# First cross attention: the mask product in 32-column tiles, and in two of eight rounds a multiplication on VectorE

## The chip, the cores and the metric

The kernel runs on one core of a Trainium2 chip. The metric is the device time of one execution in microseconds, as the median of several runs. The engines of the core are called PE (TensorE; PEld is its weight load), DVE (VectorE), ACT (ScalarE), POOL (GpSimd) and SP (the queue that issues the DMAs).

## The reference, cut to what matters

The model has two layers (cross attention, a mixing block, a feed-forward block, each twice in different forms) on 2 x 256 tokens of width 256. The change touches only the first cross attention: 256 queries of each batch attend to 4096 context rows, with 16 heads of width 16, under a mask of the form 256 x 4096 that all heads share.

```python
q = proj(q_vec, Wq, bq); k = proj(k_vec, Wk, bk); v = proj(v_vec, Wv, bv)   # 16 heads of 16
energy = einsum('bhqd,bhkd->bhqk', q, k) / sqrt(16)
energy = where(mask_input == 0, -1e9, energy)
attn = softmax(energy, axis=-1)
context = einsum('bhqk,bhkd->bhqd', attn, v)
```

A masked weight can be made in two ways: a very large negative number is added to the score ahead of the exponential, or the weight is multiplied by 0 after it. The mask of this case has only ones, so nothing is masked, but the kernel does the work for any mask.

## The kernel before, in words

`l0_xattn` (from line 153) holds the first cross attention. Its work is a software pipeline over units: one unit `u` is one batch and one pair of heads (16 units). Per unit the kernel makes two passes over the context. The first pass finds each query's largest masked score, the second makes the weights and weighs the values with them.

The main loop (from line 616) counts rounds `g`, eight per unit, and each round has two half-steps (`for a in range(2)`), one for each head of the pair. A half-step does the following, in this order on PE:

- what the generators in the list `slow` have to give: projections of keys (`project_k`, bank `psK`) and values (`project_v`, `psV`), the maxima turned into a row (`take_max`, `psM`), the division by the sum (`collect`, `psC`) and others. These are matmuls on the full 128 x 128 array. Many half-steps have none of them;
- `weights_part`, first piece (line 423): the mask product. The identity matrix `identb` (bf16) is loaded, and `addT[:, j]` (0 or -3e38 for each key and query, bf16) streams through it, so that the mask lands in PSUM bank `sts[0]`;
- `max_part` (line 408) for unit `u` and the rest of `weights_part` for the unit that is ten rounds behind, interleaved. All of these use the array in row tiles of 32 rows: the scores of the first pass into the double bank `st`, the subtraction of the maximum (line 430, a product of ones `oneb` with the three-part row `msh`) and the scores of the second pass (line 440) into two banks `sT`, one for each value of `h`, on top of the mask;
- `weigh` (line 459) for the round before: four products, one for each 32-column tile of the array, of the values with the weights `p`, into `av`.

`h` here is no head: it parts the 512 keys of a round `j` into two halves of 256. The half `h = 0` has its mask added by the mask product. The half `h = 1` has it multiplied in after the exponential: POOL multiplies `p[:, 1]` by `keep[:, j]` (line 451), and in the last ten rounds, where there is no first pass any more, DVE does it (line 449, `on_vector`).

The other engines in a half-step: ACT takes the exponential of both banks (line 446, `h = 0` first). DVE runs `max_out` (line 417), a fused add of the mask and maximum over the 128 x 1024 scores in `st`, and with it frees `st`.

What sets the order: the tile framework is told to keep each engine's instructions in the order in which the program issues them (a manual schedule), so each engine is one queue in order of the code. The buffers that couple the engines are `st` (two double banks), the pool of three single banks from which `sT` (two per half-step), `psK`, `psV`, `psM`, `psC` are taken in rotation, and `p` (five buffers).

`addT` and `keep` are made once, in the first rounds, by DVE in `make_masks` (lines 342 and 344), from mask pieces that SP loads two ahead.

Of the kernel before, what the change touches and what calls it, by code (L numbers as in the profile page):

```python
# [15 lines left out]
ALU = mybir.AluOpType  # L16
AX = mybir.AxisListType

P = 128
# [7 lines left out]
BIG = 3.0e38  # L27
# [18 lines left out]
class Kernel:  # L46
# [106 lines left out]
    def l0_xattn(self):  # L153
        nc, T, tc = self.nc, self.T, self.tc
# [95 lines left out]
        addT = a1.tile([P, NJ, 2, S], BF16, name="addT")  # L250
# [16 lines left out]
        for j in range(NJ):  # L267
# [3 lines left out]
            if j == 2:  # L271
                for f in range(2):
                    ps = self.bank("psQ")
                    for k in range(2):
                        nc.tensor.matmul(
                            ps, lhsT=wq[:, k, f * P : (f + 1) * P], rhs=self.xnT[:, k, :], start=k == 0, stop=k == 1
# [34 lines left out]
        def load_rest():  # L311
            nc.sync.dma_start(sel, T["x0_sel"])
            nc.sync.dma_start(wo, T["x0_wo"])
            self.bcast_load(bv, T["x0_bv"])
            self.bcast_load(bo, T["x0_bo"])
            nc.sync.dma_start(cw, T["a0_small"])
# [5 lines left out]
            nc.vector.memset(t, 0.0)  # L322


        NADD = 1
        none = a1.tile([P, 2], F32, name="none")

        def make_masks():
            def piece(n):
                j, h = divmod(n, 2)  # L330
                mi = a2.tile([P, 2, S], I32, name="mi", tag="mi", bufs=3)
                nc.sync.dma_start(mi, T["x0_maskT"][:, j, 2 * h : 2 * h + 2])
                return mi

            ahead = [piece(0), piece(1)]
            for n in range(2 * NJ):
                j, h = divmod(n, 2)
                if n + 2 < 2 * NJ:
                    ahead.append(piece(n + 2))
                yield  # L340
                if h == 0:
                    nc.vector.tensor_scalar(addT[:, j], ahead[n], 0, -BIG, ALU.is_equal, ALU.mult)
                else:
                    nc.vector.tensor_scalar(keep[:, j], ahead[n], 0, None, ALU.not_equal)

            for qc in range(2):
                nc.vector.tensor_reduce(
                    none[:, qc : qc + 1], madd[:, qc].rearrange("p c h a k -> p (c h a k)"), AX.X, ALU.max
                )
                yield  # L350
            nc.vector.tensor_scalar(none, none, -1.0, None, ALU.is_lt)
# [63 lines left out]
        def max_out(st, mx, par, qc, c):  # L415
            junk = a2.tile([P, 2, 512], BF16, name="junk", tag="junk", bufs=1)
            nc.vector.tensor_tensor_reduce(  # L417
                out=junk, in0=st, in1=madd[:, qc, c].rearrange("p h a k -> p h (a k)"), scale=1.0, scalar=-1e38,
                op0=ALU.add, op1=ALU.max, accum_out=mx[:, 2 * qc + par, c : c + 1],
            )  # L420

        def weights_part(qz, kst, msh, par, j, p, sts, on_vector):
            nc.tensor.matmul(  # L423
                sts[0], lhsT=self.identb, rhs=addT[:, j].rearrange("p a q -> p (a q)"), start=True, stop=False,
                skip_group_check=True,
            )
            yield
            for h in range(2):
                r = 64 * h + 32 * par
                nc.tensor.matmul(  # L430
                    sts[h], lhsT=oneb[r : r + 3, :], rhs=msh[r : r + 3, :].unsqueeze(1).to_broadcast([3, 2, S]),
                    start=h >= NADD, stop=False, tile_position=(r, 0), skip_group_check=True,
                )
            yield
            for a in range(2):
                for i in range(2):
                    for h in range(2):
                        r = 64 * h + 32 * par
                        n0 = j * S + a * P
                        nc.tensor.matmul(  # L440
                            sts[h][:, a * S : (a + 1) * S], lhsT=kst[r : r + 32, n0 : n0 + P], rhs=qz[r : r + 32, i, :],
                            start=False, stop=i == 1, tile_position=(r, 0), skip_group_check=True,
                        )
                yield
            for h in range(2):
                nc.scalar.activation(p[:, h].rearrange("p a q -> p (a q)"), sts[h], AF.Exp)  # L446

            if on_vector:
                nc.vector.scalar_tensor_tensor(p[:, 1], p[:, 1], BIG, keep[:, j], ALU.min, ALU.mult)
            else:  # L450
                nc.gpsimd.tensor_tensor(p[:, 1].bitcast(I32), p[:, 1].bitcast(I32), keep[:, j], ALU.mult)  # L451

        def weigh(av, vf, p, hp, par, j):

            for h in range(2):
                for a in range(2):
                    c = 32 * (2 * h + a)
                    o = ((2 * h + a) * H + 2 * hp + par) * VD
                    nc.tensor.matmul(  # L459
                        av[c : c + 32, :], lhsT=vf[:, o : o + 32], rhs=p[:, h, a, :],  # L460
                        start=j == 0 and par == 0, stop=j == NJ - 1, tile_position=(0, c), skip_group_check=True,
                    )
# [91 lines left out]
        NU = B * NP  # L554
        mx, msh, avs, vf, cxo, pt = {}, {}, {}, {}, {}, {}
        av = self.ps3.tile([P, 2, S], F32, name="av", tag="av")

        def chain(gens):
            for g in gens:
                yield from g  # L560
# [36 lines left out]
        def masks():  # L597
            yield from rest_of_mask()
            yield from make_masks()
# [17 lines left out]
        for g in range(8 * NU + 12):  # L617
            u, i = divmod(g, 8)
            if i == 0 and u + 1 < NU:
                load_q(u + 1)  # L620
                load_k(u + 1, 0, NJ)
            if g == 12:
                load_rest()
            if g == 14:
                slow.append(second_batch())
            if g == 8 * NU - 28:
                self.begin_rest(slow, load_weight, load_row)
            if g == 8 * NU - 6:
                self.begin_first(slow)
            if g == 8 * NP + 4:  # L630
                slow.append(second_values())
            if g in (7 * NP, 13 * NP):
                slow.append(find_base(g // (8 * NP)))
            if u >= 1 and u <= NU and i == 0:
                msh[u - 1] = a2.tile([P, S], BF16, name="msh", tag="msh")
                slow.append(take_max(u - 1, mx[u - 1], msh[u - 1]))
            if u < NU and i == 0:
                mx[u] = self.sm.tile([P, 4, 4], F32, name="mx0", tag="mx0")
            u2, j = divmod(g - 10, 8)
            u3, j3 = divmod(g - 11, 8)  # L640

            for a in range(2):
                for s in list(slow):
                    if next(s, slow) is slow:
                        slow.remove(s)
                gens = []
                for n in ([a] if u < NU else [0, 1] if a == 0 else []) if 0 <= u2 < NU else []:
                    p = pt[u2, j, n] = a2.tile([P, 2, 2, S], F32, name="p", tag="p", bufs=5)
                    if u < NU or n == 0:
                        sts = [self.bank("sT") for _ in range(2)]  # L650
                    else:
                        pair = self.bank2("st")
                        sts = [pair[:, h, :] for h in range(2)]
                    part = weights_part(qz[u2], kst[u2], msh[u2], n, j, p, sts, u >= NU)
                    next(part)
                    gens.append(part)
                if u < NU:
                    st = self.bank2("st")
                    gens = [max_part(st, qz[u], kst[u], 1 - a, *divmod(i, 4)), *gens]
                interleave(*gens)  # L660
                if u < NU:
                    max_out(st, mx[u], 1 - a, *divmod(i, 4))
                if 0 <= u3 < NU:
                    b3, hp3 = divmod(u3, NP)
                    if j3 == 0 and a == 0:
                        avs[u3] = lk.tile([P, 2, S], F32, name="avs", tag="avs")
                    weigh(av[:, a, :], vf[b3, j3], pt.pop((u3, j3, a)), hp3, a, j3)
                    if j3 == NJ - 1:
                        (nc.vector.tensor_copy if u3 == NU - 1 and a else nc.scalar.copy)(avs[u3][:, a, :], av[:, a, :])  # L669
                        if a == 1:  # L670
                            todo = [collect(avs[u3], b3, hp3)]
                            if hp3 >= NP - 2:
                                todo.append((most_heads if hp3 == NP - 2 else last_heads)(b3))
                            slow.append(chain(todo))
# [1278 lines left out]
```

## Time and profile before

| | |
|---|---|
| median of 3 runs | 1053.68 us (1049.66 to 1055.73) |
| the profiled execution | 1050.14 us, its span 1048.4 us |
| mean granted PE clock in it | 0.965 |
| DVE `max_out`, L417 | 256 of 1223 ns, 313.0 us busy |
| POOL `keep` multiplication, L451 | 236 of 1285 ns, 302.7 us busy |
| ACT exponential, L446 | 492 of 595 ns, 267.2 us busy |
| PE mask product, L423 | 246 of 394 ns, 96.8 us busy |
| DVE `keep` multiplication, L449 | 20 of 687 ns, 13.4 us busy |

The first half-step's `st` begins at 47 us, the first mask product is seen at 91.5 us, the last half-step with a `max_out` begins at 590 us, and the weighing ends at 627 us. What follows is the rest of the first layer and the second layer, which the change does not touch.

How to read the rows: a row of the timeline gives the start in us from the start of the span, the time in us, the engine, the line of the kernel, the operation, the tiles written and read, the shapes, and how many instructions of one kind were put together. In brackets stands how long the engine was idle before it, and what ended that. "issue" is time in which the engine waited for nothing that the profile shows. A matmul's time holds its passage through the array, so that the times of matmuls which follow each other overlap. A few matmul records can be missing.

### The profile page before, as it was taken

How to read it: one execution, taken by the hardware profiler on the slowest of the kernel's cores; microseconds unless marked ns; L12 is line 12 of the kernel's file. 1: busy time of each engine (PE TensorE's matmuls, PEld its weight loads, DVE VectorE, ACT ScalarE, POOL GpSimd, SP SyncE). 2: the span in 40 equal slices, each digit the busy share in tenths (PEclk: the TensorE clock that was granted, in tenths of full speed). 3: DMA queues.
4: the chain of work that ended last, by engine and by line, in shares of the span. 5: the costliest groups of instructions: out<-in, count | busy, mean ns of one | idle time of the engine just before them, and what ended most of it. 6: DMA issues, size and time to landing. Idle time of an engine off the chain costs nothing.

```text
span 1048.4 us, 21101 instructions
## 1 busy us (share of the span) xinstructions
PE 966.5 (92%) x8384; PEld 581.7 (55%) x8390; DVE 672.3 (64%) x1315; ACT 480.1 (46%) x1009; POOL 386.8 (37%) x418
## 2 busy tenths in 40 slices
PE   6998899999999999999999989764999999997978
PEld 2654355555555665555555547543575676455745
DVE  3268956666677447777887797668565432877651
ACT  1533456666666344666566672223141121455511
POOL 3323477777777435777777400111000000000000
PEclk9998799999999999999999999986899999999999
DMA  8888344334432240222221009432253796000000
GB/s 290 265 246 269 100 113 122 109 95 131 112 92 49 65 126 27 51 53 52 52 62 42 2 3 366 160 102 83 79 178 94 249 410 211 1 1 1 1 1 21
DMA packets 57523, 117.57 MB, mean 112 GB/s; under 512 B 6224, under 2 KB 28880, under 8 KB 55376
## 3 DMA queue, kind: packets, MB, share of 16 engines
q1 hardware_dynamic: 57424, 116.22, 35.8%
q8 instruction: 66, 1.08, 0.4%
q14 instruction: 33, 0.27, 0.1%
HBM read 97.85 MB, written 18.35 MB: 111 GB/s over the span
## 4 chain that ended last, share of the span: by engine, by line
PE 81%; DVE 12%; ACT 2%; issue 2%; DMA 2%; POOL 1%; SPq 0%; POOLq 0%; DVEq 0%; ACTq 0%
PE av L459 12%; PE st L408 10%; PE sT L440 8%; PE sT L423 6%; PE psV L365 6%; PE psS L1339 5%; PE psK L201 5%; PE av L1371 5%; PE psP L1456 3%; DVE junk L417 2%; PE psC L472 1%; PE psO L1581 1%; PE psP L807 1%; PE psS L1504 1%; PE psT L1379 1%
## 5 line engine op out<-in xcount | busy, mean ns | idle before, releaser
L417 DVE CUSTOM_DVE_ANT_0 junk<-st,madd 128x1024 bf16<-128x1024 f32 x256 | 313.0, 1223 | 97.1 <-PE st L408 94.5
L451 POOL TENSOR_TENSOR p<-p,keep 128x512 int32<-128x512 int32 x236 | 302.7, 1285 | 135.5 <-ACT p L446 130.0
L446 ACT ACTIVATE p<-sT 128x512 f32<-128x512 f32 x492 | 267.2, 595 | 180.0 <-PE sT L440 169.0
L440 PE MATMUL sT<-qz,kst 32*128 32x256 f32 x1968 | 207.1, 328 | 0.0
L408 PE MATMUL st<-kst,qz 32*128 32x512 f32 x1024 | 190.6, 450 | 7.5 <-DVE mx L417 7.5
L459 PE MATMUL av<-p,v 128*32 128x256 f32 x2048 | 168.0, 395 | 3.3 <-ACT avs L669 2.4
L440 PEld LDWEIGHTS sT<-qz,kst 32*128 32x128 f32 x1968 | 155.7, 189 | 0.2
L408 PEld LDWEIGHTS st<-kst,qz 32*128 32x128 f32 x1024 | 78.0, 186 | 83.8 <-issue 64.2
L104 POOL TENSOR_TENSOR rsx<-ve,nhalf 128x1 f32<-128x1 f32 (+1 forms) x10 | 5.7, 574 | 276.8 <-DVE ve L103 276.8
L430 PE MATMUL sT<-msh,oneb 3*128 3x512 bf16 x492 | 100.4, 390 | 0.5 <-ACT msh L402 0.2
L423 PE MATMUL sT<-addT,identb 128*128 128x512 bf16 x246 | 96.8, 394 | 0.2 <-ACT p L446 0.2
L201 PE MATMUL psK<-ctx,wkv 128*128 128x512 f32 x128 | 66.4, 650 | 6.6 <-DMA ctx<-in_ctxT 6.6
L423 PEld LDWEIGHTS <-identb 128*128 128x128 bf16 x256 | 25.4, 101 | 80.2 <-issue 79.1
L188 POOL TENSOR_TENSOR part<-kf,part 128x512 f32<-128x512 f32 x32 | 41.9, 1309 | 70.2 <-DVE part L187 67.7
L459 PEld LDWEIGHTS av<-p,v 128*32 128x32 f32 x2048 | 42.9, 108 | 41.6 <-ACT avs L669 3.3
L365 PE MATMUL psV<-wkv,ctx 128*128 128x256 f32 x256 | 61.8, 389 | 0.0
L1371 PE MATMUL av<-w,pT 128*128 128x256 f32 x256 | 60.3, 381 | 1.1 <-ACT pT L1383 1.1
L1339 PE MATMUL psS<-w,qk 128*128 128x512 f32 x128 | 57.8, 603 | 0.0
L365 PEld LDWEIGHTS psV<-wkv,ctx 128*128 128x128 f32 x256 | 46.7, 190 | 15.0 <-issue 9.2
L187 DVE TENSOR_SCALAR part<-kf 128x512 int32<-128x512 int32 x32 | 13.6, 426 | 61.4 <-ACT kf L205 27.9
L1371 PEld LDWEIGHTS av<-w,pT 128*128 128x128 f32 x256 | 46.4, 190 | 7.3 <-ACT pT L1383 2.1
L205 ACT ACTIVATE kf<-psK,bqk 128x512 f32<-128x512 f32 x32 | 22.0, 688 | 51.7 <-PE psK L201 51.7
(308 smaller groups left out, 1265.8 us busy)
## 6 DMA issues: line engine op xcount, KB each, us to landing
ks<-part SPq DMA_DIRECT2D x64, 256.0 KB, 2.9
w<-in_m_w SPq DMA_DIRECT2D x32, 512.0 KB, 7.7
kst<-ks SPq DMA_DIRECT2D x30, 512.0 KB, 6.6
ctx<-in_ctxT SPq DMA_DIRECT2D x24, 512.0 KB, 4.6
w<-in_ctxT SPq DMA_DIRECT2D x16, 512.0 KB, 5.7
w<-in_ctx SPq DMA_DIRECT2D x16, 512.0 KB, 4.0
qz<-qs SPq DMA_DIRECT2D x64, 64.0 KB, 6.2
mi<-in_x_maskT SPq DMA_DIRECT2D x16, 256.0 KB, 4.2
```

The lines of the kernel that those rows point to most:

```text
L201: nc.tensor.matmul(ps, lhsT=w[:, 0, k, f * P : (f + 1) * P], rhs=ct[:, k, :], start=k == 0, stop=k == 1)
L365: nc.tensor.matmul(ps[:, i, :], lhsT=ct[:, k, n0 : n0 + P], rhs=w[:, 1, k, :], start=k == 0, stop=k == 1)
L408: nc.tensor.matmul(st[:, h, :], lhsT=qz[r : r + 32, i, qc * P : (qc + 1) * P], rhs=kst[r : r + 32, c * 512 : (c + 1) * 512], start=i == 0, ...
L417: nc.vector.tensor_tensor_reduce(out=junk, in0=st, in1=madd[:, qc, c].rearrange("p h a k -> p h (a k)"), scale=1.0, scalar=-1e38, op0=ALU. ...
L423: nc.tensor.matmul(sts[0], lhsT=self.identb, rhs=addT[:, j].rearrange("p a q -> p (a q)"), start=True, stop=False, skip_group_check=True,)
L430: nc.tensor.matmul(sts[h], lhsT=oneb[r : r + 3, :], rhs=msh[r : r + 3, :].unsqueeze(1).to_broadcast([3, 2, S]), start=h >= NADD, stop=Fals ...
L440: nc.tensor.matmul(sts[h][:, a * S : (a + 1) * S], lhsT=kst[r : r + 32, n0 : n0 + P], rhs=qz[r : r + 32, i, :], start=False, stop=i == 1, ...
L446: nc.scalar.activation(p[:, h].rearrange("p a q -> p (a q)"), sts[h], AF.Exp)
L451: nc.gpsimd.tensor_tensor(p[:, 1].bitcast(I32), p[:, 1].bitcast(I32), keep[:, j], ALU.mult)
L459: nc.tensor.matmul(av[c : c + 32, :], lhsT=vf[:, o : o + 32], rhs=p[:, h, a, :], start=j == 0 and par == 0, stop=j == NJ - 1, tile_positio ...
L1339: nc.tensor.matmul(ps[:, h, :], lhsT=qk[:, k, t * P : (t + 1) * P], rhs=ctxT[t // 2][2 * i + h][:, k, :], start=k == 0, stop=k == 1,)
L1371: nc.tensor.matmul(av, lhsT=pT[:, c, :], rhs=cn[t // 2][i][:, c, :], start=i + c == 0, stop=i == 7 and c == 3)
```

## The change

The mask product (line 423) is issued as four matmuls instead of one. Each loads 32 columns of the identity into one of the four column tiles of the array, streams the same `addT[:, j]`, and writes 32 of the 128 partitions of `sts[0]`. It stands at the same place in the program.

In the rounds `j` = 2 and 6 of each unit there is no mask product. In these rounds `addT[:, j]` holds 1 or 0 instead of 0 or -3e38, the product of line 430 opens the bank of `h = 0`, and DVE multiplies `p[:, 0]` by `addT[:, j]` after the exponential (`mask_first`). That multiplication is issued behind the half-step's `max_out`. In the last ten rounds of the loop, which do the `keep` multiplication on DVE, it goes back to POOL in the rounds `j` = 2 and 6.

```diff
+        FACTOR = (2, 6)
...
                 if h == 0:
-                    nc.vector.tensor_scalar(addT[:, j], ahead[n], 0, -BIG, ALU.is_equal, ALU.mult)
+                    if j in FACTOR:
+                        nc.vector.tensor_scalar(addT[:, j], ahead[n], 0, None, ALU.not_equal)
+                    else:
+                        nc.vector.tensor_scalar(addT[:, j], ahead[n], 0, -BIG, ALU.is_equal, ALU.mult)
...
         def weights_part(qz, kst, msh, par, j, p, sts, on_vector):
-            nc.tensor.matmul(
-                sts[0], lhsT=self.identb, rhs=addT[:, j].rearrange("p a q -> p (a q)"), start=True, stop=False,
-                skip_group_check=True,
-            )
+            for c in range(0, 0 if j in FACTOR else P, 32):
+                nc.tensor.matmul(
+                    sts[0][c : c + 32, :], lhsT=self.identb[:, c : c + 32],
+                    rhs=addT[:, j].rearrange("p a q -> p (a q)"), start=True, stop=False, tile_position=(0, c),
+                    skip_group_check=True,
+                )
             yield
...
-                    start=h >= NADD, stop=False, tile_position=(r, 0), skip_group_check=True,
+                    start=h == 1 or j in FACTOR, stop=False, tile_position=(r, 0), skip_group_check=True,
...
-            if on_vector:
+            if on_vector and j not in FACTOR:
                 nc.vector.scalar_tensor_tensor(p[:, 1], p[:, 1], BIG, keep[:, j], ALU.min, ALU.mult)
             else:
                 nc.gpsimd.tensor_tensor(p[:, 1].bitcast(I32), p[:, 1].bitcast(I32), keep[:, j], ALU.mult)
+
+        def mask_first(p, j):
+            if j in FACTOR:
+                nc.vector.scalar_tensor_tensor(p[:, 0], p[:, 0], BIG, addT[:, j], ALU.min, ALU.mult)
...
                     max_out(st, mx[u], 1 - a, *divmod(i, 4))
+                for n in [n for m, k, n in pt if (m, k) == (u2, j) and (n == a or u >= NU and a == 0)]:
+                    mask_first(pt[u2, j, n], j)
```

More of the change, by code (lines that the diff above doesn't have):

```diff
@@ L322, in l0_xattn @@
             nc.vector.memset(t, 0.0)
-        NADD = 1
+        FACTOR = (2, 6)
         none = a1.tile([P, 2], F32, name="none")
```

## The prediction

> **What bounds the kernel now.** I read the page first (busy shares, the chain that ended last), then the table of 20 us windows, then the timeline of single half-steps (a half-step is one pass of the `for a` loop), last the records where an engine waits.
>
> ```profile
> PE 966.5 (92%) x8384; PEld 581.7 (55%) x8390; DVE 672.3 (64%) x1315; ACT 480.1 (46%) x1009; POOL 386.8 (37%) x418
> ...
> PE 81%; DVE 12%; ACT 2%; issue 2%; DMA 2%; POOL 1%; SPq 0%; POOLq 0%; DVEq 0%; ACTq 0%
> ```
>
> ```profile
> 80.00:100.00 20.00, 16.62 (x105) 8.74 (x105) 17.61 (x32) 6.73 (x14) 6.45 (x12) 0.79 0.92 279
> 460.00:480.00 20.00, 20.00 (x274) 11.19 (x275) 14.64 (x27) 12.14 (x23) 14.91 (x17) 1.00 0.03 7
> 520.00:540.00 20.00, 20.00 (x274) 10.66 (x269) 17.43 (x31) 12.93 (x25) 15.17 (x17) 1.00 0.01 2
> ```
>
> (PE, PEld, DVE, ACT, POOL busy, granted clock, DMA.) From about 130 to 592 us TensorE is never idle at full clock. Only near 80 to 120 us does VectorE set the pace. One undisturbed half-step:
>
> ```profile
> 464.26 0.64 PE L459 MATMUL av<-p,v 128*32 128x256 f32 x8
> 464.43 1.09 ACT L446 ACTIVATE p<-sT 128x512 f32<-128x512 f32 x2 [0.60 <-PE sT L440]
> 464.83 0.10 PEld L423 LDWEIGHTS <-identb 128*128 128x128 bf16 x1 [0.41 <-issue]
> 464.84 0.39 PE L423 MATMUL sT<-addT,identb 128*128 128x512 bf16 x1
> 465.15 0.18 PEld L408 LDWEIGHTS st<-kst,qz 32*128 32x128 f32 x2 [0.23 <-issue]
> 465.16 0.39 PE L430 MATMUL sT<-msh,oneb 3*128 3x512 bf16 x2
> 465.65 1.27 POOL L451 TENSOR_TENSOR p<-p,keep 128x512 int32<-128x512 int32 x1 [0.41 <-ACT p L446]
> 465.93 1.23 DVE L417 CUSTOM_DVE_ANT_0 junk<-st,madd 128x1024 bf16<-128x1024 f32 x1 [0.46 <-PE st L408]
> 465.95 0.16 PEld L459 LDWEIGHTS av<-p,v 128*32 128x32 f32 x8
> 466.12 1.08 ACT L446 ACTIVATE p<-sT 128x512 f32<-128x512 f32 x2 [0.60 <-PE sT L440]
> ```
>
> The period is 465.95 - 464.26 = 1.69 us, in three parts with three array shapes: weighing in 32-column tiles 0.57, the mask product on the full array 0.32, the row-tiled scores 0.80. The loads at 464.83 and 465.15 stood 0.41 and 0.23 us for "issue": each is the first load of a new shape and starts only when the stream before it is out.
>
> **Cost of the mask product now.** Behind the weighing 0.32 us (464.83 to 465.15). Behind full-array work (value projection, `psV`) less:
>
> ```profile
> 378.65 0.81 PE L365 MATMUL psV<-wkv,ctx 128*128 128x256 f32 x3
> 379.30 0.38 PE L423 MATMUL sT<-addT,identb 128*128 128x512 bf16 x1
> 379.61 0.49 PE L408 MATMUL st<-kst,qz 32*128 32x512 f32 x2
> ```
>
> `psV` matmuls start every 0.216 us, the mask follows in step, and the scores come 0.31 after it, of which 0.216 is its stream. So a change of shape costs 0.31 - 0.216 = about 0.09, and the product is worth 0.216 here, 0.32 behind the weighing.
>
> **Column tiles (six of eight rounds).** Shape as in the weighing, so the change of shape between the two goes. In the weighing's records the second set of four starts 0.24 after the first (staggered by 0.02); four mask tiles should do the same. Scores then start 0.02 + 0.216 + 0.09 + 0.24 = 0.57 after the weighing's second set began, against 0.65 now: 0.08 saved. By the predecessor of each mask product in the trace, 106 half-steps of these rounds follow the weighing at the 1.69 period: 106 x 0.08 = 8.5 us. Where full-array work stands between (35: 8 `psK`, 10 `psV`, 14 `psC`, 3 others) the shape now changes twice: 0.09 more and the stagger 0.02, 35 x 0.115 = 4.0 lost. Fourteen with `psM` between wait for ScalarE anyway (below): 0. Net 4.5 saved.
>
> A rule speaks against this. The Trainium skill (TensorEngine Tiling (Array Packing), Restrictions) has column tiling switch off Fast Weight Load, and its TensorE: Matmul & The Clock Gate (LDWEIGHTS) prices a load at columns/1.2 GHz: by estimate 27 ns per tile, 0.107 for four if they lie in the open. That makes 0.08 saved into 0.03 lost, 106 x 0.03 = 3 us slower. The row shows eight 32-column loads busy 0.16 us together at 465.95, started within 0.05 us, the later four under running matmuls. I take the row.
>
> **Factor rounds (2 and 6).** The product goes: TensorE gains 0.32 behind the weighing, 0.216 behind other work. But `sT` rotates through three banks and a half-step takes two, so its second score group (`oneb`, h = 1) needs the bank that the previous half-step's first Exp has read. Now Exp ends 0.14 before that matmul in undisturbed half-steps; where it is late the wait is seen:
>
> ```profile
> 451.30 1.09 ACT L446 ACTIVATE p<-sT 128x512 f32<-128x512 f32 x2 [0.61 <-PE sT L440]
> 452.27 0.54 PE L430 MATMUL sT<-msh,oneb 3*128 3x512 bf16 x2
> 453.28 1.08 ACT L446 ACTIVATE p<-sT 128x512 f32<-128x512 f32 x2 [0.63 <-PE sT L440]
> ```
>
> The pair of `oneb` matmuls takes 0.54 instead of 0.39: the second started at 452.44, 0.05 after Exp ended (451.30 + 1.09). From there to the next Exp's start is 0.84, its first half 0.60, waking 0.05: a loop of 1.49 that no gain on TensorE shortens. TensorE alone would give 1.37; I take 1.50. So 43 factor half-steps at 1.69 save 0.19, 8.2 us; 11 behind full-array work save 0.216, 2.4; four others about 0.2, 0.8. Sum 11.4. Column rounds, at 1.61, stay above the loop.
>
> **What is added.** One VectorE multiply of p's first half per factor half-step, 64 in all, behind `max_out`, ahead of the next `max_out`. Nearest in form: L449, same operation on 128x512, 687 ns. Nearest in place, two SBUF inputs right behind `max_out`:
>
> ```profile
> 578.08 0.69 DVE L751 TENSOR_TENSOR fw<-fw,fr 128x512 f32<-128x512 f32 x1
> 578.35 2.97 POOL L451 TENSOR_TENSOR p<-p,keep 128x512 int32<-128x512 int32 x2 [1.32 <-ACT p L446]
> 578.68 1.22 DVE L417 CUSTOM_DVE_ANT_0 junk<-st,madd 128x1024 bf16<-128x1024 f32 x1
> ```
>
> VectorE is not held; GpSimd's first multiply takes 1.56 (with the next, 2.97) instead of 1.28, so 0.28 is lost; half-steps stay at 1.69. The Trainium skill (SBUF — State Buffer, Who interferes with whom) says a VectorE operation with two SBUF inputs and a GpSimd operation that reads SBUF exclude each other, the later one blocked to the end. By the rule GpSimd loses its whole overlap, 0.42; by the row 0.28. More matters who is first: L342's `addT` fill, usually 0.42, took 1.39 where GpSimd had begun 0.17 before it.
>
> Cover, from the records: `max_out` ends a median 1.39 us before its `st` buffers are wanted, the `keep` multiply 0.73 before weighing. In a pair of factor half-steps (first row phase at 0, second at 1.49) the multiply runs 1.92 (its Exp is done at 1.56) to 2.61, `keep` 2.19 to 3.75; the second at 3.67 waits 0.1, ends 4.4; its `keep` ends near 5.5, 0.56 late, with 0.56 of cover left at the new pace. Undisturbed pairs therefore cost 0. If that cover fails, each lost tenth costs TensorE a tenth. Queued behind the multiply is only `max_out`, which then runs 0.6 late against 1.2 of cover. Where projections put split subtractions (1.31 each) on GpSimd, about 160 to 340 us with 13 pairs, it lags: bounds 0 (found free) and 1.3 (held by one `keep`) less the cover, 0.6; half are caught, 0.3 x 13 = 4 us. In the two pairs near 102 and 124 us VectorE leads: bounds 0 (it idles 0.65 and 0.86 for mask loads) and 4 x 1.3; I take 2.5. The `addT` fills change one operand: 0. In the tail GpSimd, idle there, takes over three rounds' `keep`, VectorE gets as many multiplies: 0. The DMAs stay. Later stages only begin earlier.
>
> **Sum** against the profiled execution (1050.1 us, span 1048.4): 4.5 + 11.4 - 4 - 2.5 = 9.4 saved, 1040.7. The runs' median, 1053.7, is 3.6 higher: forecast 1044.
>
> **Rivals.**
> *Full gain (0.16).* The Exp loop isn't binding and the stalls don't come: 43 x 0.32 = 13.8 instead of 8.2; 4.5 + 17.0 - 2 = 19.5, 1034. Against: the 0.54 above.
> *Nothing (0.13).* Column loads lie open: -3 - 4 instead of +4.5, so 11.4 - 7 - 6.5 = -2.1, 1056. Against: the load row.
> *Slower (0.17): lock order.* If the pair's second multiply comes after the first `keep` has ended (3.75 against my 3.67), the second `keep` goes first, to 5.03. The multiply ends at 5.7, the next `max_out` starts 1.9 late against 1.2 of cover: 0.7 stalled. 28 pairs: 19.6. Sum 15.9 - 2.5 - 19.6 = -6, 1060. It decides at 0.08 us, a margin smaller than what side jobs on VectorE shift; for me speaks a `xn` fill at 538.28 that came 0.62 into one GpSimd multiply and still went before the next (0.95 us in all).
> *The tiles don't run together (0.01)*: 192 x 0.64 us, 1177. The weighing excludes it.
>
> **Numbers.** The likeliest case (0.53) is 1044, own range 1038 to 1050. A measurement of this kernel tells 0.5%, 5 us, from no change. Faster by more: most of the first case and the full gain, 0.63; same 0.16; slower, the lock order and a worse early stage, 0.21. The range 1031 to 1060 leaves out the ends.
>
> **To see afterwards.** Half-steps at 1.61 in column rounds and 1.50 in factor rounds; no "issue" wait of 0.41 ahead of the `identb` loads behind the weighing, one behind `psV`; multiplies of 0.69 to 0.8, not 1.3 to 2; few waits of `st` for VectorE or of `av` for GpSimd. Rounds at 1.69 still, or multiplies over 1.3, would prove me wrong.

## The result and the profile after

The changed kernel takes 1063.03 us (median of 4 runs, 1062.12 to 1067.40) where the kernel before takes 1052.68 (4 runs). It is 10 us slower by the medians; the ratio over all these runs is 1.011, 95% interval 1.0078 to 1.0141. The prediction was 1044, faster. The profiled execution took 1062.61 us, its span 1060.8, the mean granted clock 0.954 (before 0.965).

The page of the kernel after, the chain that ended last by engine, and one of the costliest groups:

```profile
PE 70%; DVE 16%; POOL 4%; issue 4%; ACT 3%; DMA 2%; SPq 0%; POOLq 0%; DVEq 0%; ACTq 0%
...
L458 POOL TENSOR_TENSOR p<-p,keep 128x512 int32<-128x512 int32 x242 | 326.8, 1358 | 144.3 <-ACT p L453 125.6
```

PE's share of the chain fell from 81 to 70%, and DVE and POOL went from 13 to 20: the bound is shared now. The `keep` multiplication on POOL went from a mean of 1285 ns to 1358. In the records, 53 of the 242 take over 1.4 us, before 8 of 236. DVE's new multiplications themselves are hardly touched: 55 of 67 take at most 0.80 us, 7 over 1.1. (There are 67 and not 64: in the last ten rounds the list that feeds `mask_first` takes the second head of a factor round in both half-steps, so that three of them are multiplied twice. The result is the same, but in the tail the weighing waits twice, 1.8 and 1.4 us, for such a second multiplication.) PE's records of waiting show the other half:

```profile
PEld st L412 <- DVE mx L421: 35.9, 39, 4.8
```

(Sum in us, number, longest.) The loads of the scores waited 16.1 us for `max_out` before, now 35.9, the matmuls 7.5 and now 15.9.

The column tiles did what they were put in for. One undisturbed column half-step, from the timeline:

```profile
467.79 0.49 PE L412 MATMUL st<-kst,qz 32*128 32x512 f32 x2
...
468.59 0.64 PE L470 MATMUL av<-p,v 128*32 128x256 f32 x8
...
468.83 0.12 PEld L429 LDWEIGHTS <-identb 128*32 128x32 bf16 x4
...
469.37 0.50 PE L412 MATMUL st<-kst,qz 32*128 32x512 f32 x2
```

From scores to scores it is 469.37 - 467.79 = 1.58 us (1.58 to 1.59 elsewhere; before 1.69), and the load of `identb` no longer stands 0.41 for "issue". By the single records the weighing's second set begins at 468.83, so the scores follow 0.54 after it instead of 0.65: about 0.11 saved, 0.08 forecast.

The loss is elsewhere. Here is a pair of factor half-steps (round 6) and the row of maxima after it:

```profile
447.41 0.60 PE L437 MATMUL sT<-msh,oneb 3*128 3x512 bf16 x2
...
449.00 0.51 PE L437 MATMUL sT<-msh,oneb 3*128 3x512 bf16 x2
...
449.36 0.69 DVE L462 SCALAR_TENSOR_TENSOR p<-p,addT 128x512 f32<-128x512 f32 x1
449.45 0.68 POOL L388 CAST parts<-nm 128x8 bf16<-128x8 f32 x1
...
450.71 0.39 PE L437 MATMUL sT<-msh,oneb 3*128 3x512 bf16 x2
...
451.12 0.68 DVE L462 SCALAR_TENSOR_TENSOR p<-p,addT 128x512 f32<-128x512 f32 x1
451.19 4.22 POOL L458 TENSOR_TENSOR p<-p,keep 128x512 int32<-128x512 int32 x3
...
452.99 0.14 PEld L470 LDWEIGHTS av<-p,v 128*32 128x32 f32 x4 [1.33 <-POOL p L458]
...
454.10 0.39 PE L437 MATMUL sT<-msh,oneb 3*128 3x512 bf16 x2
```

Two things are to be seen. First, POOL lies under DVE: a CAST of 8 columns that takes 0.22 us alone takes 0.68, because it starts 0.09 after a multiplication and ends 0.08 after it; the `keep` that starts at 451.19, 0.07 after the second multiplication, took 1.74 instead of 1.28. That is 0.46 twice. In the half-step that begins at 450.71 the weighing then stands for POOL, and that half-step takes 3.39 us. Second, the half-step at 447.41 to 449.00 took 1.59, not 1.50: the pair of `oneb` matmuls spreads over 0.60 (0.39 in a column round), the sign of the wait for the previous Exp.

The first point holds far beyond this place. In after, 60 POOL operations (`keep` multiplications, CASTs and small subtractions) begin while a new multiplication runs. Each takes longer than its usual 1.28, 0.22 or 0.20 us by the time that the multiplication still had to go, less 0.13 to 0.16 us. Together that is 22.6 us of POOL's time.

Where the time went, by stages of the profiled executions (us, from the records of `st` and `av`; half-steps are counted from the first `st`, the tail runs from the last `st` to the last weighing; in brackets the time at half clock; the experiments are described below):

| kernel | to first `st` | half-steps 0-32 | 32-112 | 112-160 | 160-255 | tail | rest | span |
|---|---|---|---|---|---|---|---|---|
| before | 47.0 | 76.8 (20.5) | 174.5 (3.4) | 120.3 | 171.1 | 38.1 | 420.5 (45.5) | 1048.4 |
| after | 45.3 | 75.8 (17.1) | 174.7 (6.8) | 124.2 (3.4) | 173.0 (3.4) | 45.0 (12.4) | 422.9 (54.3) | 1060.8 |
| columns only | 45.4 | 74.5 (13.7) | 174.8 (13.7) | 122.9 (2.6) | 165.2 (0.8) | 38.4 | 426.4 (59.2) | 1047.6 |
| factor, no multiplication | 45.5 | 73.0 (14.4) | 170.5 (9.5) | 120.3 (1.4) | 168.9 (12.3) | 44.9 (10.3) | 421.0 (55.7) | 1044.0 |
| columns behind weighing | 45.3 | 75.7 (20.5) | 172.0 (6.8) | 120.8 (3.4) | 163.6 | 38.0 | 420.4 (45.5) | 1035.8 |

The changed kernel has lost 3.9 us in half-steps 112 to 160, 1.9 in those after, 6.9 in the tail and 2.4 in the rest, and won 2.7 ahead of half-step 32. The brackets matter when two kernels are compared: at half clock a half-step of 1.58 us takes 2.41 (factor without multiplication, near 410 us), so by estimate a third of such time is lost where PE sets the pace. A second count therefore leaves out every half-step from 20 to 254 that either of two kernels spent in part at half clock (203 to 221 of 235 are left):

| from | to | us |
|---|---|---|
| before | columns only | -8.2 |
| columns only | factor, no multiplication (e3) | -5.4 |
| e3 | after | +14.3 |
| e3 | half the first Exp (e9) | -4.5 |
| e3 | one-input operation (e11) | +2.3 |
| after | same operation, written elsewhere (e12) | +1.2 |

So ahead of the tail the factor rounds gain 5.4 us and their multiplication takes 14.3.

### The profile page after: what moved, and what is told of

Same layout as the page of the kernel before. It is cut to its first block, busy times and chain, and to the rows that moved or that the text cites. A ratio compares the mean times of both kernels' runs of the same rounds, so it can differ in the third digit from the quotient of the medians.

```text
span 1060.8 us, 22174 instructions
## 1 busy us (share of the span) xinstructions
PE 963.5 (91%) x8902; PEld 594.3 (56%) x8902; DVE 724.0 (68%) x1376; ACT 479.7 (45%) x1009; POOL 417.1 (39%) x424
## 4 chain that ended last, share of the span: by engine, by line
PE 70%; DVE 16%; POOL 4%; issue 4%; ACT 3%; DMA 2%; SPq 0%; POOLq 0%; DVEq 0%; ACTq 0%
PE av L470 9%; PE st L412 8%; PE sT L447 6%; PE psS L1352 5%; PE psV L369 5%; DVE junk L421 5%; PE av L1384 5%; PE psK L201 5%; PE sT L429 3%; PE psP L1469 3%; POOL p L458 2%; PE psC L483 1%; ACT p L453 1%; PE psO L1594 1%; PE psT L1564 1%
## 5 line engine op out<-in xcount | busy, mean ns | idle before, releaser
L458 POOL TENSOR_TENSOR p<-p,keep 128x512 int32<-128x512 int32 x242 | 326.8, 1358 | 144.3 <-ACT p L453 125.6
L447 PE MATMUL sT<-qz,kst 32*128 32x256 f32 x1968 | 210.6, 330 | 0.0
L412 PE MATMUL st<-kst,qz 32*128 32x512 f32 x1024 | 193.8, 457 | 16.0 <-DVE mx L421 15.9
L470 PE MATMUL av<-p,v 128*32 128x256 f32 x2048 | 178.0, 404 | 12.8 <-DVE p L462 4.9
L447 PEld LDWEIGHTS sT<-qz,kst 32*128 32x128 f32 x1968 | 158.1, 192 | 0.3
L412 PEld LDWEIGHTS st<-kst,qz 32*128 32x128 f32 x1024 | 81.1, 188 | 122.7 <-issue 72.1
L437 PE MATMUL sT<-msh,oneb 3*128 3x512 bf16 x492 | 108.4, 392 | 0.3 <-DVE mean L877 0.2
L429 PE MATMUL sT<-addT,identb 128*32 128x512 bf16 x740 | 78.2, 393 | 0.4 <-ACT p L453 0.4
L470 PEld LDWEIGHTS av<-p,v 128*32 128x32 f32 x2048 | 44.7, 110 | 57.7 <-POOL p L458 9.8
L201 PE MATMUL psK<-ctx,wkv 128*128 128x512 f32 x128 | 64.0, 630 | 6.7 <-DMA ctx<-in_ctxT 6.7
L462 DVE SCALAR_TENSOR_TENSOR p<-p,addT 128x512 f32<-128x512 f32 x67 | 53.0, 793 | 0.8 <-ACT p L453 0.8
```

The costliest lines, as they stand in the source:

```text
L201: nc.tensor.matmul(ps, lhsT=w[:, 0, k, f * P : (f + 1) * P], rhs=ct[:, k, :], start=k == 0, stop=k == 1)
L412: nc.tensor.matmul(st[:, h, :], lhsT=qz[r : r + 32, i, qc * P : (qc + 1) * P], rhs=kst[r : r + 32, c * 512 : (c + 1) * 512], start=i == 0, ...
L429: nc.tensor.matmul(sts[0][c : c + 32, :], lhsT=self.identb[:, c : c + 32], rhs=addT[:, j].rearrange("p a q -> p (a q)"), start=True, stop= ...
L437: nc.tensor.matmul(sts[h], lhsT=oneb[r : r + 3, :], rhs=msh[r : r + 3, :].unsqueeze(1).to_broadcast([3, 2, S]), start=h == 1 or j in FACTO ...
L447: nc.tensor.matmul(sts[h][:, a * S : (a + 1) * S], lhsT=kst[r : r + 32, n0 : n0 + P], rhs=qz[r : r + 32, i, :], start=False, stop=i == 1, ...
L470: nc.tensor.matmul(av[c : c + 32, :], lhsT=vf[:, o : o + 32], rhs=p[:, h, a, :], start=j == 0 and par == 0, stop=j == NJ - 1, tile_positio ...
```

## The experiments

Theory A (after the result): the multiplication on DVE and the multiplication on POOL hold each other up, POOL loses, and the weighing waits for it where nothing covers that. Rival B: the factor rounds themselves bring nothing, because Exp and the banks pace them. Rival C: the column tiles cost more behind full-array work than they gain. All edits are to the changed kernel. Ratios are to the kernel before.

### The two parts apart

**Columns only** (e1): all eight rounds have column tiles.

```diff
-        FACTOR = (2, 6)
+        FACTOR = ()
```

> Only the column tiles, in all eight rounds; no factor rounds. Theory A (the factor rounds' VectorE multiplication is the loss, and the column tiles gain): undisturbed half-steps at 1.59 us as in the changed kernel, 11 us below before, about 1042. Rival B (the column tiles are the loss, because behind full-array work the shape of the array changes twice): at or above before, 1053 or more.

Measured: 1048.74 us, ratio 0.994 (0.991 to 0.997). Some 6 of the 11 us forecast came, but the tiles are a gain alone, so C is no explanation of the loss; the factor rounds turn 6 us won into 10 lost.

**Factor only** (e2): the six other rounds have the full-array product of before.

```diff
-            for c in range(0, 0 if j in FACTOR else P, 32):
-                nc.tensor.matmul(sts[0][c : c + 32, :], lhsT=self.identb[:, c : c + 32], ...)
+            if j not in FACTOR:
+                nc.tensor.matmul(sts[0], lhsT=self.identb, ...)
```

> Factor rounds as in the changed kernel, but the mask product of the other six rounds on the full array again. Theory A: the multiplication's cost stays and little is gained, 1060 (1056 to 1064), slower than before. Rival B: the gain of the factor rounds stays without the loss, 1045 or less.

Measured: 1070.09, ratio 1.019 (1.014 to 1.023), slower as theory A had it, though above its range of 1056 to 1064. The tiles of six rounds are worth 1.019 - 1.011 = 0.8% here, some 8 us, with the intervals of both on it: the two parts nearly add up.

**One factor round of four** (e6: `FACTOR = (2,)`; e7: `FACTOR = (6,)`).

> The changed kernel with one factor round of eight, the one that lies far from the making of the row of maxima (round 2). If the loss comes mostly from round 6, whose multiplications lie at the same half-steps as the six small GpSimd operations that make that row: 1050. If each factor round costs the same: 1055.

> The same with round 6 alone. If round 6 is the worse: 1059 and the half-step with the row of maxima at 3.4 us as in the changed kernel. If each factor round costs the same: 1055.

Measured: 1052.38, ratio 0.998 (0.995 to 1.001), and 1057.32, ratio 1.006 (1.003 to 1.009). Both lie between their two forecasts. Against columns only, round 2 costs 0.4% and round 6 costs 1.2%. They do the same work at different places: round 6 lies where `take_max` puts six small operations on POOL. The half-step with `psM` that follows (at unit 8) took 1.93 us before, 2.36 with columns only, 2.37 with round 2 as a factor, and 3.39 with round 6 and with both. It is not so in every unit: over units 4 to 15 of after this half-step takes from 1.94 to 3.73.

### What of the factor rounds costs

**No multiplication** (e3), **no `keep` in factor rounds** (e4). Each takes one partner of the suspected meeting away.

```diff
         def mask_first(p, j):
+            return
```

```diff
-            else:
+            elif j not in FACTOR:
                 nc.gpsimd.tensor_tensor(p[:, 1].bitcast(I32), ... keep[:, j], ALU.mult)
```

> The changed kernel without the new multiplication on VectorE: in the factor rounds the mask of the first half is left out. Theory A: all of the loss goes, and because each half-step is held at 1.59 us by the chain from the row of ones over the first Exp to the next row of ones, it comes out within 3 us of the kernel with column tiles only: 1041. Rival C (TensorE alone sets the pace in factor rounds, at 1.37 us each): 64 x 0.2 = 13 us lower than that kernel, 1029.

> The changed kernel without the keep multiplication in the factor rounds: there the mask of the second half is left out, so that the new multiplication meets fewer GpSimd multiplications. If it is the meeting of the two[...] that costs: most of the loss goes, 1045. If it is VectorE's own time for 64 multiplications: 1057 or more.

Measured: e3 1045.78, ratio 0.994 (0.991 to 0.996); e4 1045.85, ratio 0.995 (0.993 to 0.997). Either partner's absence takes off all 17 us, though in e4 all of DVE's multiplications are still there and in e3 all of POOL's; from half-step 32 to 255 e4 takes 459.2 us, e3 459.7, after 471.9. So neither engine's load alone is the cost: it takes both. e3 ends 3 us from columns only, as theory A had it, though at 1046 and not 1041. In e3 the place shown above reads:

```profile
442.96 0.22 POOL L388 CAST parts<-nm 128x8 bf16<-128x8 f32 x1
...
444.23 1.28 POOL L458 TENSOR_TENSOR p<-p,keep 128x512 int32<-128x512 int32 x1
```

CAST and `keep` are back at 0.22 and 1.28, and the half-step with `psM` takes 2.47. The difference to the 3.39 of after is 0.92, twice 0.46 (in e4 it takes 1.94). Over units 2 to 15 this half-step is 5.3 us longer in after than in e3. From e3 to after the stages grow by 2.8, 4.2, 3.9 and 4.1 us before the tail, 0.1 in it.

That is one part of it. At full clock 7.1 of the 14.3 us lie in the two half-steps of round 3, behind the pair of round 2, and there it is DVE that comes late. In after:

```profile
526.44 0.68 DVE L462 SCALAR_TENSOR_TENSOR p<-p,addT 128x512 f32<-128x512 f32 x1
526.66 1.60 POOL L458 TENSOR_TENSOR p<-p,keep 128x512 int32<-128x512 int32 x1 [0.15 <-ACT p L453]
527.04 1.50 DVE L887 TENSOR_SCALAR fw<-fw 128x512 f32<-128x512 f32 x1
```

The multiplication holds the `keep`, and the `keep`, now 0.32 later, holds DVE's next operation, a side job that takes 0.42 us alone. `max_out` starts behind it, and the scores stand 1.5 us for `max_out`. Between half-steps 20 and 255 of after, 31 operations of DVE lose 21.9 us under a `keep` against their usual times; in e3 9 lose 5.6, in e4 12 lose 6.4. So the two engines hold each other up, as theory A has it, but POOL is not the only one that loses.

e3 speaks for B as well. Its ratio is that of columns only: in the runs, two rounds without any mask product gain nothing over two rounds with one. By stages e3 is 4.8 us ahead of columns only at half-step 255 and gives 6.5 back in the tail.

**Another operation of the same length** (e11): a maximum over `p[:, 0]`, one SBUF input, nothing of `p` written.

```diff
-                nc.vector.scalar_tensor_tensor(p[:, 0], p[:, 0], BIG, addT[:, j], ALU.min, ALU.mult)
+                gone = self.sm.tile([P, 2], F32, name="gone", tag="gone")
+                nc.vector.tensor_reduce(gone, p[:, 0], AX.X, ALU.max)
```

> The changed kernel with the new multiplication replaced by a maximum over the same 128x512 of p into two columns: as long on VectorE (0.68 us), in the same place of its queue and with the same wait, but with one SBUF input, and weighing doesn't wait for it (the mask of the first half in factor rounds is left out). If VectorE's time is the cost: 1063. If meeting GpSimd[...], and weighing's wait for it, is the cost: near the kernel without the multiplication, 1047.

Measured: 1053.89, ratio 1.000 (0.996 to 1.005), between the two forecasts. With 0.68 us on DVE in the same place, `keep` has a mean of 1287 ns, the first CAST takes 0.22 and the half-step with `psM` 2.46. So what holds POOL is the form of the operation, not a busy DVE. The form differs in two points, the second SBUF input and the full product written. `max_out` settles which: it writes a full product too, but reads one input from SBUF and one from PSUM, and beside 256 of them `keep` has its 1285 ns before. For an operation that would hold POOL, that leaves the second input.

Only 9 of the 17 us go in this run, but at full clock it is 2.3 us over e3, where after is 14.3. The rest of what remains goes with more time at half clock (26.2 us between 130 and 590 us, e3 13.7, after 7.4) and with the tail (47.6 us), which this run does not explain.

**The same operation, written elsewhere** (e12), to part the lock from the weighing's wait for the product:

```diff
-                nc.vector.scalar_tensor_tensor(p[:, 0], p[:, 0], BIG, addT[:, j], ALU.min, ALU.mult)
+                gone = a2.tile([P, 2, 512], BF16, name="junk", tag="junk", bufs=1)
+                nc.vector.scalar_tensor_tensor(gone[:, 0]..., p[:, 0], BIG, addT[:, j], ALU.min, ALU.mult)
```

> The multiplication on VectorE keeps its form, its two SBUF inputs and its place, but writes its product into the scratch tile of max_out, so that the weighing no longer waits for it (the first half's mask is left out of the result). Against the 1063 of the kernel after and the 1054 with a one-input operation in its place. If the meeting with GpSimd costs the time: 1060 to 1063, keep multiplications still with a mean near 1.36 us and the half-step with psM in round 6's wake still near 3.4 us. If the weighing's wait for the multiplication costs it: 1052 to 1055, that half-step near 2.47.

Measured: 1077.39, ratio 1.024 (1.020 to 1.028), outside both. The edit brought a wait of its own: multiplication and `max_out` now write the same scratch tile, so each starts only when the other has ended. Below, the multiplication starts 0.11 us after the end of `max_out`'s last record (454.25 + 0.08), where after has it 0.08 ahead of that end, 0.19 later in all; the next `max_out` follows 0.15 after the multiplication's end.

```profile
453.79 4.20 POOL L458 TENSOR_TENSOR p<-p,keep 128x512 int32<-128x512 int32 x3
...
454.25 0.08 DVE L421 DVE_READ_ACCUMULATOR2_ANT mx<- 128x1 f32 x1
454.44 1.17 DVE L463 SCALAR_TENSOR_TENSOR junk<-p,addT 128x512 bf16<-128x512 f32 x1
```

The `keep` came first, and now DVE is held: 1.17 instead of 0.69, with the next `max_out` behind it. The size follows the same sum as above: the first `keep` had 0.62 to go, 0.48 was lost. 23 of 67 multiplications take over 1.1 us (after: 7), and the scores wait 49.4 and 19.4 us for `max_out`. So a multiplication that comes 0.2 us later often comes second, as the rival "lock order" in the prediction had it. The wait of the weighing is no explanation of POOL's loss: without it `keep` still has a mean of 1354 ns. At full clock e12 is 1.2 us over after, so most of the 14 us go with the time at half clock (35.7 us between 130 and 590); why there is more of it stays open. As the edit made a new wait, this run doesn't part the two costs cleanly; e3, e4 and e11 carry the argument.

### Why the factor rounds gain nothing

**Half the first Exp** (e9): e3 with the first exponential over 256 of its 512 columns, the weighing taking those twice.

```diff
-            for h in range(2):
-                nc.scalar.activation(p[:, h]..., sts[h], AF.Exp)
+            nc.scalar.activation(p[:, 0, 0], sts[0][:, 0:S], AF.Exp)
+            nc.scalar.activation(p[:, 1]..., sts[1], AF.Exp)
```

> The changed kernel without the new multiplication (the mask of the first half in factor rounds is left out), and with the first Exp over 256 of its 512 columns (the other 256 weights of the first half are left out, the first 256 stand in for them). If the chain through the first Exp holds all rounds at 1.59: factor half-steps come at 1.37 both, 43 x 0.2 = 9 us below the kernel without the multiplication alone, 1037; column rounds stay near 1.57, which is TensorE's own pace. If the chain doesn't bind: 1046, the same.

Measured: 1038.81, ratio 0.987 (0.981 to 0.992). The same pair of half-steps:

```profile
441.55 0.39 PE L437 MATMUL sT<-msh,oneb 3*128 3x512 bf16 x2
...
442.92 0.39 PE L437 MATMUL sT<-msh,oneb 3*128 3x512 bf16 x2
...
444.51 0.39 PE L437 MATMUL sT<-msh,oneb 3*128 3x512 bf16 x2
```

With the short Exp, `oneb` is 0.39 again and the two steps into and inside the pair take 1.38 (from 440.17) and 1.37 us, which was the prediction's figure for TensorE alone; the next stays at 1.59. With the whole Exp (e3, after) the same three take 1.37, 1.59 and 1.71, together 4.67, against 3 x 1.585 = 4.76 with column tiles: 0.09 gained per pair. At full clock e9 is 4.5 us ahead of e3, in the runs 7. So the wait for Exp takes most of what the factor rounds would gain, and B is shown for undisturbed half-steps: little is left, not nothing.

### Where it is lost otherwise

**The last rounds on DVE as before** (e8): both multiplications on DVE in the last ten rounds.

```diff
-            if on_vector and j not in FACTOR:
+            if on_vector:
```

> The changed kernel, but in the last ten rounds VectorE does both multiplications also in factor rounds, so that no GpSimd multiplication meets it there. If the longer tail (43.9 us from the last maximum to the last weighing, against 37.8) comes from meeting GpSimd: 1058, 5 us below the changed kernel. If it comes from VectorE's load: 1063 or more.

Measured: 1063.16, ratio 1.012 (1.007 to 1.016). The first forecast failed and the second fits: the tail takes 44.7 us, as in after, with no `keep` on POOL in its factor rounds. But DVE's load isn't the only way to lose there. Without the first multiplication (e3) the tail takes 44.9 too, and it takes 38.9 where factor rounds have no `keep` (e4). In e8 DVE has five multiplications of 0.68 us in a factor round of the tail, where before it has two. In e3 the `keep` that went back to POOL meets other work of DVE:

```profile
599.47 1.88 DVE L843 SCALAR_TENSOR_TENSOR u<-big,cw,u 128x256 f32<-128x256 f32 x2
...
599.71 2.76 POOL L458 TENSOR_TENSOR p<-p,keep 128x512 int32<-128x512 int32 x2 [14.45 <-ACT p L453]
601.27 1.68 DVE L533 TENSOR_TENSOR cxo<-cxo,base 128x448 f32<-128x448 f32 x1
...
603.10 0.66 PE L527 MATMUL psX<-ident,cxo 128*128 128x128 f32 x2 [3.58 <-DVE cxo L533]
```

In columns only the same two DVE rows take 0.88 and 0.62, and `psX` waits 1.06 us. So here POOL comes first, DVE is held in operations that the change doesn't touch, and PE stands 3.58 us; from 602.4 its clock is at half. After has both: three multiplications on DVE and two on POOL in a factor round of the tail. From 600 to 620 us it does 216 matmuls at a mean granted clock of 0.83, columns only 290 at 1.00. Of its tail 12.4 us are at half clock, before none.

**The maxima on DVE** (e10): `take_max`'s small operations off POOL.

```diff
-            eng = nc.vector if u == NU - 1 else nc.gpsimd
+            eng = nc.vector
```

> The changed kernel with the six small operations that make the row of maxima on VectorE in all units, where GpSimd had them in all but the last. If the 3.4 us half-step comes from these operations lying between the keep multiplications on GpSimd: back to about 2.4, 15 x 1.0 less, 1050. If VectorE's queue is what is late there: 1063 or more.

Measured: 1105.3, ratio 1.050 (1.045 to 1.055). The first forecast failed, and the second gave no size for such a loss. The mean clock is 0.923, with 77.4 us at half clock between 130 and 590 us. The small operations meet `keep` on DVE as well. Here a `keep` runs from 469.10 to 470.38:

```profile
469.16 1.27 DVE L388 CAST parts<-nm 128x8 bf16<-128x8 f32 x1
```

The CAST takes 0.18 alone. 23 of 48 take over 0.5 us, and `max_out` lies behind them: the scores wait 65.5 and 31.4 us for it. The long half-step is now the one ahead of `psM`, with a median of 3.5 us and up to 4.7. So a second SBUF input isn't the only form of DVE's operations that meets `keep`: this CAST has one.

### What a better version keeps

**Column tiles only behind the weighing** (e5): no factor rounds. Where a generator of `slow` took a PSUM bank in this half-step, the mask product is the one full-array matmul of before.

```diff
-        FACTOR = (2, 6)
+        FACTOR = ()
...
+                before = self.taken
                 for s in list(slow):
                     if next(s, slow) is slow:
                         slow.remove(s)
+                between = self.taken > before
...
+            if between:
+                nc.tensor.matmul(sts[0], lhsT=self.identb, ...)
-            for c in range(0, 0 if j in FACTOR else P, 32):
+            for c in range(0, 0 if between else P, 32):
```

(`self.taken` counts in `bank` and `bank2`.)

> No factor rounds; column tiles only where the mask product directly follows the weighing, the full array where a projection, the row of maxima or the division stands between. If the second change of shape costs 0.1 us in about 45 half-steps, as the prediction had it: 4 us below the kernel with column tiles everywhere, 1044, and half-steps behind values at 3.51 again. If it costs nothing: 1048, no change.

Measured: 1037.37, ratio 0.984 (0.980 to 0.988). It beats both kernels, by the ratios some 17 us under before and 28 under after, and gains more than the 4 us forecast. Behind a value projection, columns only and then this version:

```profile
355.64 1.99 PE L369 MATMUL psV<-wkv,ctx 128*128 128x256 f32 x8
...
359.27 1.99 PE L369 MATMUL psV<-wkv,ctx 128*128 128x256 f32 x8
```

```profile
352.88 2.00 PE L372 MATMUL psV<-wkv,ctx 128*128 128x256 f32 x8
...
356.39 1.78 PE L372 MATMUL psV<-wkv,ctx 128*128 128x256 f32 x7
```

3.63 against 3.51 us from one projection to the next: behind full-array work the tiles cost 0.12, where they save about 0.11 behind the weighing. 66 mask products of this version have such work in front, by estimate 6 to 8 us at 0.09 to 0.12 each. Up to the last weighing it is 5.9 us ahead of columns only (615.4 us against 621.3), with 31 us at half clock in both. The rest of the 11 us between the two versions lies after the first attention (426.4 us against 420.4), where the code is the same and the time at half clock is 59.2 us against 45.5; whether the version has a part in that isn't shown.

## Why the prediction was wrong

**Column tiles, 0.08 x 106 = 8.5 less 35 x 0.115 = 4.0.** Right in kind, sign and size. The saving is about 0.11, the price 0.11 to 0.12. The load row held against the estimate from what the Trainium skill states (TensorEngine Tiling (Array Packing), Restrictions: column tiling disables Fast Weight Load): four loads, busy 0.12 us, stand under running matmuls. The price of the 35 was written down and not used: e5 is that line of the sum turned into a kernel.

**Factor rounds, "I take 1.50", 11.4 saved.** Right in mechanism, wrong in its reach. The loop from `oneb` through Exp to the next `oneb` was read at a half-step that already stood, with 0.84 us from the second `oneb` to Exp. In a half-step that starts on time it is 0.95, so the first step of a pair has a loop of 0.95 + 0.60 + 0.05 = 1.60, a column round's own pace. From second `oneb` to second `oneb` the medians are 1.60 into the pair, 1.49 inside it and 1.58 behind it, so the loop that was forecast for all factor half-steps holds for one in two. Against column tiles in the same rounds, 9.9 us were forecast (11.4 less 1.5 for two rounds of tiles); measured are 4.8 us up to half-step 255 (columns only against e3) and 0 in the runs, since the tail gives it back.

**"Undisturbed pairs therefore cost 0."** Failed, and this is the largest single miss. Early pairs were put at 2.5 and the 160 to 340 us region at 4; from e3 to after the first two stages (to 296 us) grow by 2.8 and 4.2. The two stages behind, put at 0, grow by 3.9 and 4.1, the last although e3 has 9 us more at half clock in it; at full clock the multiplication takes 14.3 in all. The cover came from medians over all half-steps, 0.73 us for `keep`. The multiplication of round 6 stands where POOL also has six small operations. Before, the half-step with `psM` two later took 1.93; the shorter half-steps alone make it 2.36 (columns only), so the cover was already gone. On top, DVE holds a CAST and a `keep` for 0.46 each. Behind the multiply were queued not only `max_out`, as the prediction had it, but DVE's side jobs too, and these meet the late `keep`: round 2's share of the loss.

**Who loses.** The row at 578 us (0.28 lost) and the rule of the Trainium skill (SBUF — State Buffer, Who interferes with whom: the later one blocked to the end) were weighed as two prices, 0.28 and the whole overlap of 0.42. They are one: the later operation loses what the earlier one still has to go, less 0.14. That gives 0.28 in the row of before, 0.46 for the CAST here (multiplication to 450.05, CAST from 449.45), and in e12 and e10 the same for DVE behind `keep`. The price was right and the place was not: the new multiplications mostly meet POOL at the start of its operation, with 0.6 to go. The rival "lock order" named 1060. Its mechanism, DVE held with `max_out` behind it, is rare for the multiplications of after (7 of 67; e12 made it 23), but common for the side jobs.

**Tail 0.** Failed: 6.9 us. GpSimd did stand idle, but the tail has no cover. DVE, ACT and PE work there in turns, DVE gets nine multiplications and not six, and the three rounds' `keep` on POOL hold DVE's other work, as e3 shows. How much of the 6.9 is the clock's is open.

**The sum.** Forecast were 9.4 us saved: 6.0 by tiles in all rounds, 9.9 more by the factor rounds over them, less 6.5 for the multiplication. Up to half-step 255 the profiled runs show 6.8 saved by the tiles (before to columns only), 4.8 more without the multiplication (e3) and 14.8 lost with it (after). The tail loses 6.9, and the rest of the kernel, which nothing was forecast for, 2.4 with 9 us more at half clock: together, to rounding, the 12.4 us by which the span grew. One reading was off as well: PE is not busy throughout from 130 to 592 us; in the 20 us from 400 it was busy 18.24. It changes no term.

## What to carry to other kernels

Read the cover of a new operation at the very place where it is put, among the small operations of both engines that hold each other up, and after the rest of the change has shortened the cycle; a median over the pipeline says nothing of it. Time a loop between engines at a step that runs unstalled, since a stalled step hides its own first part (0.84 us here instead of 0.95). A matmul with a choice of array shape should take the shape of the work in front of it, case by case.

## What the hardware showed beyond that

Spells at half clock, in lengths of about 3.4 us and multiples (3.4, 6.8, 10.2, 13.7), came into the middle of the first attention, where a half-step of 1.58 then takes 2.41. The Trainium skill (TensorE: Matmul & The Clock Gate, What's actually happening) has a window of that length in which the array's activity is judged, and these lengths agree. They come back at the same places of the program: one begins at half-step 214 (506 to 549 us) in e2, e4, e6, e7, e8, e10, e11 and e12, in after a short one six half-steps later, and in none of before, columns only, e3, e5 and e9; another at half-step 158 or 159 in columns only, e3, e5, e6, e9, e10 and e11. They last 3.4 to 13.7 us, of which by the estimate above a third is lost. Over the whole span before has 75 us at half clock, after 99, e12 140, e10 170. What trips them at these places isn't settled. Columns only alone ranged from 1038 to 1054 us over 20 runs, its mean clock from 0.963 to 0.951.
